# The order of two small matmuls on TensorE in a two-layer graph network: the mask's counting matmul and layer 1's second matmul

## The chip, the cores and the metric

The kernel runs on one core of one Trainium2 chip. The metric is the device time of one execution in microseconds. Of the kernel before there are three timed runs; the profile is one execution recorded by the hardware profiler.

## What is computed

128 batches of 128 nodes with 64 features go through two graph layers, each followed by a residual and a layer norm:

```python
# layer 0
mask = (adj > 0.0)
h   = relu((x @ W1a)[:, :, None, :] + (x[:, :, None, :] - x[:, None, :, :]) @ W1b + b1)   # (b, j, k, 192)
hm  = einsum('bjkh,bjk->bjh', h, mask)
x   = layernorm(x + hm @ W2 + mask.sum(-1)[..., None] * b2)
# layer 1
agg = einsum('bmn,bnd->bmd', adj, x)
h   = elu(agg @ V1 + c1)        # 64 -> 128
h   = elu(h @ V2 + c2)          # 128 -> 128
x   = layernorm(x + h @ V3 + c3)
```

About 6% of the mask's entries are set, so layer 0 doesn't have to look at all 128 x 128 pairs of nodes of a batch.

## The kernel before, in words

**Tiling.** Two batches are handled together as a pair p; there are 64 pairs and so 64 rounds. For each pair the nodes are sorted by their number of neighbours. The sorted nodes are cut into nine blocks with 7 to 22 slots per node, and each block is one unit of work: ScalarE writes a start value into a PSUM bank (L910), TensorE adds the neighbours' projections with 18 small matmuls (the gather, L920), and VectorE reduces the slots with absolute values (L930). Four banks `e0` to `e3` serve the units.

**The steps around the units.** Everything else of a pair is written as Python generators, whose steps yield an engine, a modelled cost, the events they need, and how many small PSUM banks they take:

- `turn` and `project_c` transpose the inputs and project the neighbours; the copy out of `turn`'s bank is `turned` (L695, ScalarE).
- `prepare` counts degrees and ranks the nodes. Its last step `permute` (L575, VectorE) frees its bank.
- `sort_x` and `project_a` sort the node features and project them (L606, TensorE); three ScalarE instructions write `aj` out of that bank (L613).
- `sort_mask` sorts the mask with a matmul, copies it as `mtp` (L659) and the permutation as `permT` (L661), then comes the counting matmul: `prefix` times `mtp` (L664 to L666; the helper `stationary`, L248, issues it), which numbers the set entries along each row. ScalarE copies the result as `vp` (L668), and VectorE compares it with slot numbers to make the one-hot tiles `oh` (L675) that the gather reads.
- `finish` is the rest of both layers of a pair: `hm` (L842), `project` (L847 and L851), the copy `ys` (L855), `unsort` (L864), a norm, `aggregate` (L871), layer 1's first matmul `hidden1` (L880), an elu (`r` L791, `e` L794, `h` L797), layer 1's second matmul `hidden2` (L886), a second elu, and `last` (L891 to L893) with the second norm.

**What sets the order.** The class `Flow` writes all engines' instructions out in one order. While the units run (all but the last 14 of 576), it always takes the runnable step with the smallest due time; a step is runnable when the steps that it needs have been written out and enough banks are free. The due times are in the table `DUE`: for pair p, a step's due time is `ROUND * p` plus its entry, with `ROUND = 11.1651`. Steps of several pairs so interleave in a fixed cycle. The entries of `sort_mask` are, in order, the sorting matmul, `mtp`, `permT`, the counting matmul, `vp`, and the nine `oh`. Those of `finish` have `hidden2` at 43.31 and the `r` behind it at 43.44.

In the last 14 units, and before the first gather, the step that can start first by the modelled clocks is taken, and due times only decide between near ones.

**Banks.** The small matmuls share four PSUM banks `m0` to `m3`. `give` appends a bank to a list when the step that reads it out has been written, and a matmul takes the first of the list:

```python
args = [self.free.pop(0)[1] for _ in range(banks)]
```

A matmul that writes a bank must wait on the chip until the instruction that last read it has ended. The framework puts these waits in by itself from the order of the instructions.

**PE mode.** A step marked `PE:*` follows the mode that TensorE is in: after a gather (mode "t") `stationary` issues two half-width matmuls, otherwise one of 128 columns.

Of the kernel before, what the change touches and what calls it, by code (L numbers as in the profile page):

```python
# [47 lines left out]
def gnn_kernel(ctx: ExitStack, tc: tile.TileContext, x, adj, w1, b1, w2, b2,  # L48
# [28 lines left out]
    with ExitStack() as fast:  # L77
        loads = fast.enter_context(tc.tile_pool(name="loads", bufs=8))
        prep = fast.enter_context(tc.tile_pool(name="prep", bufs=5))
        work = fast.enter_context(tc.tile_pool(name="work", bufs=5))  # L80
        ps_e = fast.enter_context(tc.tile_pool(name="ps_e", bufs=1, space=bass.MemoryType.PSUM))
        ps_m = fast.enter_context(tc.tile_pool(name="ps_m", bufs=1, space=bass.MemoryType.PSUM))
        K = sparse(tc, locals())
# [103 lines left out]
def sparse(tc, env):  # L187
# [17 lines left out]
    DUE = {  # L205
        "prepare": (-43.06, -42.93, -39.21, -39.08, -35.87),
        "sort_x": (-26.76, -10.46, -10.33, -3.14, -3.02, 2.5, 2.63, 2.76, 2.89),
        "sort_mask": (-26.12, -25.99, -25.86, -23.42, -23.29, -23.16, -13.67, -13.28, -13.03,
                      -12.77, -2.63, -2.25, -1.99, -1.73),
        "turn": (-36.9, -36.77),  # L210
        "project_c": (-32.15, -29.32, -29.2, -29.07, -28.94, -4.17, -4.04),
# [967 lines left out]
```

## Time and profile before

| | |
|---|---|
| timed runs, us | 758.67, 760.54, 761.2 |
| median, us | 760.54 |
| span of the profiled execution, us | 758.2 |
| its mean granted TensorE clock | 0.988 |
| the counting matmul (L248 with `prefix`), 64 times, mean ns | 273 |
| layer 1's second matmul (L886), 128 records for 64 steps, mean ns | 421 |
| copy `vp` (L668), 64 times, mean ns | 373 |

The span runs from the first to the last instruction of the program. The profiled execution is recorded apart from the list of times, and no time besides its span is given for it. FP32 matmuls appear as two records each, with a weight load before each. The end of a matmul in the profile is modelled, so successive matmuls seem to overlap; the starts tell more than the durations. PE is TensorE, PEld its weight loads, DVE VectorE, ACT ScalarE, POOL GpSimd. A line such as L248 is that of a helper, so the tile names tell the steps apart.

### The profile page before, as it was taken

The numbers are of one execution on the slowest core, as the hardware profiler recorded it, in microseconds if no ns is written. First come the engines' busy times: TensorE is split into PE (matmuls) and PEld (weight loads), VectorE is DVE, ScalarE is ACT, GpSimd is POOL, SyncE is SP. The second block draws the span as 40 slices with busy tenths as digits, with TensorE's granted clock in tenths as the row PEclk, the third lists the DMA queues.
The fourth block names the chain that finished last, engine by engine and source line by source line (L and its number), as shares of the span: only waits on it lengthen the run. The fifth ranks groups of instructions, "written<-read, shape, count | busy, mean of one in ns | idle before, by whom it ended". The sixth has DMA issues, their size and how long they took to land.

```text
span 758.2 us, 36118 instructions
## 1 busy us (share of the span) xinstructions
PE 736.3 (97%) x14788; PEld 672.4 (89%) x14789; DVE 722.5 (95%) x2381; ACT 705.7 (93%) x1986; POOL 432.4 (57%) x801
## 2 busy tenths in 40 slices
PE   7699999999999999999999999999999999999994
PEld 4588999999999999999999999999999999999993
DVE  7799999999999999999999999999999999999984
ACT  4499999999999999999999999999999999999984
POOL 5255566566556557556556656655655655655662
PEclk9799999999999999999999999999999999999998
DMA  4000011011011011011101101101101101100000
GB/s 121 15 3 3 17 31 31 17 31 32 16 31 32 20 27 31 20 27 31 28 20 31 31 17 32 31 16 31 31 20 28 31 21 27 31 21 16 10 13 19
DMA packets 54667, 19.72 MB, mean 26 GB/s; under 512 B 37600, under 2 KB 54496, under 8 KB 54496
## 3 DMA queue, kind: packets, MB, share of 16 engines
q1 hardware_dynamic: 53792, 17.05, 9.3%
q8 instruction: 118, 1.93, 1.1%
q14 instruction: 53, 0.43, 0.2%
q10 hardware_dynamic: 704, 0.30, 0.2%
HBM read 13.14 MB, written 4.19 MB: 23 GB/s over the span
## 4 chain that ended last, share of the span: by engine, by line
PE 95%; DVE 2%; ACT 1%; DMA 1%; issue 0%; POOL 0%; POOLq 0%; SPq 0%; DVEq 0%; ACTq 0%
PE e L920 46%; PE m L606 6%; PE m L708 5%; PE m L847 5%; PE m L886 4%; PE m L880 4%; PE m L893 4%; PE m L864 3%; PE m L246 3%; PE m L690 3%; PE m L592 2%; PE m L871 2%; PE m L851 1%; PE m L711 1%; PE m L248 1%; PE m L691 1%
## 5 line engine op out<-in xcount | busy, mean ns | idle before, releaser
L920 PE MATMUL e<-oh,cp 128*64 128x162 bf16 (+3 forms) x10368 | 393.3, 229 | 6.0 <-DVE oh L675 5.6
L920 PEld LDWEIGHTS <-cp 128*64 128x64 bf16 x10368 | 357.8, 110 | 18.3 <-issue 6.6
L930 DVE TENSOR_REDUCE sums<-e 128x54 f32<-128x486 f32 (+8 forms) x576 | 334.4, 608 | 10.2 <-PE e L920 4.6
L910 ACT COPY e<-aj 128x504 f32<-128x504 f32 (+6 forms) x576 | 293.6, 543 | 3.1 <-DVE sums L930 2.6
L749 POOL TENSOR_SCALAR ve<-st 128x2 f32<-128x2 f32 x126 | 24.1, 191 | 242.4 <-DVE st L742 237.0
L675 DVE TENSOR_TENSOR oh<-vp,slotc 128x308 bf16<-128x308 bf16 (+6 forms) x576 | 148.9, 315 | 4.8 <-ACT vp L668 1.3
L750 POOL TENSOR_TENSOR rs<-ve,mhalf 128x2 f32<-128x2 f32 x126 | 87.8, 697 | 10.5
L727 POOL TENSOR_TENSOR cp<-r,cp 128x512 bf16<-128x512 f32 x64 | 74.5, 1164 | 32.0 <-ACT cp L725 32.0
L642 POOL TENSOR_TENSOR corr<-ea,sa 128x384 f32<-128x384 f32 x64 | 64.3, 1005 | 16.5 <-DVE ea L635 11.5
L791 ACT ACTIVATE r<-m,cc 128x256 f32<-128x256 f32 x128 | 61.4, 480 | 5.2 <-PE m L880 3.2
L842 POOL TENSOR_TENSOR hm<-sums,corr 128x384 f32<-128x384 f32 x63 | 63.2, 1004 | 4.0 <-DVE sums L930 4.0
L620 POOL TENSOR_TENSOR sa<-aj,srow 128x384 f32<-128x384 f32 x64 | 64.3, 1005 | 1.0 <-ACT aj L613 1.0
L613 ACT ACTIVATE aj<-m,b1c 128x128 f32<-128x128 f32 x192 | 56.5, 366 | 8.2 <-PE m L606 1.2
L797 DVE SCALAR_TENSOR_TENSOR h<-m,cc,e 128x256 f32<-128x256 f32 x128 | 60.3, 471 | 2.0 <-ACT e L794 1.9
L794 ACT ACTIVATE e<-r 128x256 f32<-128x256 f32 x128 | 54.4, 426 | 2.1
L606 PE MATMUL m<-xsT,wad 128*128 128x128 f32 x384 | 53.7, 276 | 0.0
L847 PE MATMUL m<-w2d,hm 128*128 128x128 f32 x384 | 53.5, 276 | 0.0
L722 DVE TENSOR_TENSOR r<-m,cp 128x256 f32<-128x256 f32 x128 | 47.7, 414 | 1.6 <-ACT cp L718 1.6
L771 ACT ACTIVATE x<-y,nb,rs 128x64 f32<-128x64 f32 x126 | 49.0, 441 | 0.2 <-POOL nb L753 0.2
L718 ACT CAST cp<-m 128x256 bf16<-128x256 f32 x128 | 40.3, 366 | 8.8 <-PE m L711 8.8
L847 PEld LDWEIGHTS m<-w2d,hm 128*128 128x128 f32 x384 | 48.0, 192 | 0.3 <-POOL hm L842 0.3
L606 PEld LDWEIGHTS m<-xsT,wad 128*128 128x128 f32 x384 | 47.9, 192 | 0.4
(157 smaller groups left out, 1350.3 us busy)
## 6 DMA issues: line engine op xcount, KB each, us to landing
adj<-in_adj_dram SPq DMA_DIRECT2D x64, 128.0 KB, 2.9
xx<-in_x_dram SPq DMA_DIRECT2D x64, 64.0 KB, 2.6
out_dram<-o SPq DMA_DIRECT2D x64, 64.0 KB, 1.6
w1s<-in_L_gnn_W_dram ACTq DMA_DIRECT2D x2, 96.0 KB, 3.2
w2s<-in_L_gnn_W_dram ACTq DMA_DIRECT2D x2, 48.0 KB, 3.0
v2s<-in_L_gnn_W_dram SPq DMA_DIRECT2D x1, 64.0 KB, 2.2
v1d<-in_L_gnn_W_dram SPq DMA_DIRECT2D x2, 32.0 KB, 2.1
rows<-in_L_gnn_b_dram SPq DMA_DIRECT2D x1, 64.0 KB, 5.6
```

Source lines behind the costliest of these rows:

```text
L606: nc.tensor.matmul(aps[:, c * N:(c + 1) * N], wad[:, c, :], xsT, start=True, stop=True)
L620: evs, = yield ("POOL PORT", 1.0, [have] + made("srow"), 0, lambda: nc.gpsimd.tensor_mul(sa, aj, srow))
L642: ev, = yield ("POOL PORT", 1.05, [ev, evs], 0, lambda: nc.gpsimd.tensor_sub(corr, ea, sa))
L675: lambda: nc.vector.tensor_tensor(oh[:, :, c].rearrange("p b (s w) -> p b s w", w=w), vp[:, :, p0:p1].rearrange("p b (o w) -> p b o w", o= ...
L727: lambda: nc.gpsimd.tensor_sub(cp[:, 2], r1, cp[:, 1]))
L750: nc.gpsimd.tensor_tensor(rs, ve, mhalf, op=OP.pow)
L791: lambda: nc.scalar.activation(r, z, AF.Relu, bias=c, scale=-1.0))
L842: lambda: (nc.vector if late else nc.gpsimd).tensor_sub(hm, d["sums"], d["corr"]))
L847: nc.tensor.matmul(yb[:, :2 * O], hm[:, c, :], flat(w2d[:, c]), start=(c == 0), stop=False)
L910: lambda: nc.scalar.copy(e.rearrange("p (c s w) -> p c s w", c=3, w=w), d["aj"][:, :, p0:p1].rearrange("p c (o w) -> p c o w", o=1) .to_br ...
L920: nc.tensor.matmul(e[s * HB:(s + 1) * HB, c * n:(c + 1) * n], cp[:, k, s, c * HB:(c + 1) * HB], oh[:, s, base:base + n], start=False, stop ...
L930: nc.vector.tensor_reduce(d["sums"][:, :, p0:p1], e.rearrange("p (c s w) -> p c w s", c=3, w=w), AX.X, OP.add, apply_absolute_value=True)
```

## The change

One due time in the table of `sort_mask` is made smaller, that of the counting matmul:

```diff
     DUE = {
         "prepare": (-43.06, -42.93, -39.21, -39.08, -35.87),
         "sort_x": (-26.76, -10.46, -10.33, -3.14, -3.02, 2.5, 2.63, 2.76, 2.89),
-        "sort_mask": (-26.12, -25.99, -25.86, -23.42, -23.29, -23.16, -13.67, -13.28, -13.03,
+        "sort_mask": (-26.12, -25.99, -25.86, -23.75, -23.29, -23.16, -13.67, -13.28, -13.03,
                       -12.77, -2.63, -2.25, -1.99, -1.73),
```

For a pair p the counting matmul is now due at 11.1651 p - 23.75, and `hidden2` of pair p - 6 at 11.1651 p - 23.68 (43.31 - 6 x 11.1651 = -23.68). Before, it was due at 11.1651 p - 23.42, behind `hidden2` and behind that step's `r`. No other entry is changed, and no instruction is added or removed.

## The prediction

> **What bounds the kernel now.** I read the page first, then the table by windows, then the waits of the steady stretch, and last the order of time inside one round. The page:
>
> ```profile
> span 758.2 us, 36118 instructions
> PE 736.3 (97%) x14788; PEld 672.4 (89%) x14789; DVE 722.5 (95%) x2381; ACT 705.7 (93%) x1986; POOL 432.4 (57%) x801
> ...
> PE 95%; DVE 2%; ACT 1%; DMA 1%; issue 0%; POOL 0%; POOLq 0%; SPq 0%; DVEq 0%; ACTq 0%
> ```
>
> Four of five engines look full, but the chain that ended last is TensorE for 95% of the span. The windows were cut at 11.24 us, the distance from one round's instructions to the same ones of the next (64 rounds, one per pair of batches):
>
> ```profile
> 200.00:211.24 11.24, 11.24 (x238) 10.35 (x234) 11.06 (x37) 10.97 (x33) 6.65 (x13) 1.00 0.09 21
> ...
> 400.00:411.24 11.24, 11.24 (x239) 10.35 (x235) 11.07 (x37) 10.97 (x32) 6.64 (x13) 1.00 0.11 27
> ```
>
> After the length come the busy times of TensorE's matmuls (11.24 of 11.24), weight loads, VectorE, ScalarE, GpSimd, and the clock (1.00). TensorE has no free moment; VectorE has 0.17 us, ScalarE 0.27. The waits from 60 to 710 us, longest first:
>
> ```profile
> POOL ve L749 <- DVE st L742: 214.0, 57, 3.9
> POOL cp L727 <- ACT cp L725: 23.9, 58, 1.2
> PEld L711 <- issue: 19.2, 58, 0.3
> ```
>
> No matmul stands in that list. So a microsecond put on TensorE in a round is a microsecond on the span, once per round, and one taken off is won only if nothing else holds the matmul behind it. One round at the place of the change, in order of time (start, length, engine):
>
> ```profile
> 404.23 0.50 ACT L695 COPY turned<-m 128x384 f32<-128x384 f32 x1
> 404.85 0.88 ACT L613 ACTIVATE aj<-m,b1c 128x128 f32<-128x128 f32 x3
> 405.32 0.34 PE L851 MATMUL m<-cp,mtp 128*128 128x64 bf16 x6
> 405.46 0.30 PEld L886 LDWEIGHTS m<-h,v2s 128*128 128x128 f32 x2
> 405.49 0.68 PE L886 MATMUL m<-h,v2s 128*128 128x256 f32 x2
> 405.69 0.27 ACT L855 COPY ys<-m 128x128 f32<-128x128 f32 x1
> 405.79 0.10 PEld L248 LDWEIGHTS <-prefix 128*128 128x128 bf16 x1
> 406.01 0.27 PE L248 MATMUL m<-mtp,prefix 128*128 128x256 bf16 x1
> 406.01 0.52 PEld L864 LDWEIGHTS m<-ys,permT 128*128 128x128 f32 x4
> 406.12 0.56 PE L864 MATMUL m<-ys,permT 128*128 128x64 f32 x4
> 406.35 0.48 ACT L791 ACTIVATE r<-m,cc 128x256 f32<-128x256 f32 x1
> ```
>
> L886 is layer 1's second matmul (`hidden2`), L248 the counting matmul, L864 `unsort`. The same stretch in round 5, where no `hidden2` exists yet and the counting matmul already follows L851:
>
> ```profile
> 57.38 0.34 PE L851 MATMUL m<-cp,mtp 128*128 128x64 bf16 x6
> 57.53 0.10 PEld L248 LDWEIGHTS <-prefix 128*128 128x128 bf16 x1
> 57.56 0.27 PE L248 MATMUL m<-mtp,prefix 128*128 128x256 bf16 x1
> 57.76 0.27 ACT L855 COPY ys<-m 128x128 f32<-128x128 f32 x1
> 58.08 0.41 PEld L864 LDWEIGHTS m<-ys,permT 128*128 128x128 f32 x3 [0.45 <-ACT ys L855]
> ```
>
> It prices two things: the count's matmul can start about 0.03 us after L851's last, and a weight load held back by ScalarE starts 0.05 us after the ScalarE instruction ended (57.76 + 0.27 = 58.03, load at 58.08).
>
> [...] the count's load stands at 405.79 under the running L886, its matmul at 406.01, after it. So a waiting `hidden2` holds everything behind it. [...] bf16 loads of L851 come 0.03 us apart (six matmuls inside 0.17 us of the chain), L886's two FP32 loads 0.11 apart (405.46, 405.57). [...] So I reckon from starts alone.
>
> **The change part by part.** One due time moves, from -23.42 to -23.75 us of the kernel's own plan. Modulo the round of 11.1651 the counting matmul goes from 10.08 to 9.75; `hidden2` stands at 9.81, ScalarE's `r` of it at 9.94, the copy of unit 0 at 9.69. So it passes `hidden2` alone. No DMA and nothing of ScalarE, VectorE, GpSimd or SyncE changes place: `vp`, the count's eviction, stays behind `r`. The PE mode stays plain, since L847/L851 precede either way, so it stays one 128-column matmul (all 58 later records of L248 with `prefix` are). Swaps: round p against `hidden2` of p-6, so p = 6 to 63, 58 of them.
>
> *Streams.* Nothing is added or removed: `hidden2` 2 x 0.216 (its second matmul to the count's, 405.79 to 406.01), the count 0.11 (to L864's first, 406.12).
>
> *Weights.* Now `hidden2`'s first FP32 load starts behind a 64-column matmul and leaves TensorE uncovered: from 405.49 to the first L886 stream at 405.57, 0.08 us. Behind the count's 0.11 us stream the load would be covered. Gain at most 0.08. But L864's load needs `ys`, which ends at 405.96 and releases at 406.01; L864 starts its load exactly there now. So without any other effect the matmuls behind would not start earlier: 0.00 to -0.08 by itself, and I take 0.
>
> *The bank.* The four small PSUM banks are handed out first freed, first taken. The last four freed before this place are, by due time modulo the round, those of `turned` (7.89), `aj` (8.15), `ys` (8.40) and `permute` (8.79). Before, `hidden2` takes the first, the count the second. After, the count takes `turned`'s and `hidden2` takes `aj`'s. The trace supports it: L886's load and, separately, the count's matmul each wait for ScalarE's semaphore, and the second must be for something later than the first. `turned` ends at 404.23 + 0.50 = 404.73, long before either. `aj` ends at 404.85 + 0.88 = 405.73: harmless for a count at 406.01, late for a `hidden2` that would now load at 405.50. FP32 waits stand before the first weight load (L864 shows it in round 5), so the load is held too.
>
> Sum, round at 405 us:
> - the last L851 matmul starts at 405.46, the count at 405.49, its stream ends at 405.60;
> - `hidden2`'s load: 405.73 + 0.05 = 405.78;
> - first stream after the load's 0.11: 405.89; second 0.216 later: 406.11;
> - L864's first stream: 406.32 (its load at 406.11 or so, `ys` long there).
>
> Now it is 406.12. Cost about 0.207 us a round (unrounded starts), 0.19 if the release took 0.03, 0.22 if another hundredth or two comes on top. `aj` itself waits for TensorE (its PE source L606 ends right before it), so it moves with TensorE's clock and the loss repeats; it doesn't wear off.
>
> *Who waits behind.* On TensorE: L864, L880, the gathers of unit 8 and 0, all by 0.207. On ScalarE `r` starts now at 406.35, 0.18 after L886's modelled end (405.79 + 0.38); afterwards that end is 406.11 + 0.38 = 406.49, so `r` starts near 406.52, 0.16 late, less than TensorE's shift. `vp` behind it and `oh` on VectorE move by the same 0.16. Neither gains a stall against TensorE; both get slack.
>
> 58 x 0.207 = 12.0 us on the profiled span: 758.2 to 770.2. The fastest of the runs shown, 758.67, lies 0.5 above the span, the median of 760.54 2.3 above; the profiled execution is not marked among them. I add to the median: 772.5. In the last unit rounds (the final 14 units of 576) the order follows modelled ready times and could change a little; I put ±1 us on it.
>
> **Rivals.**
> *No bank wait, slack holds* (ends on the other side: not slower). If the banks went the other way round, or `aj` were free by 405.45, the swap would only hide the load. For: 0.08 us of uncovered load is really there. Against: `ys` pins L864 at 406.01, so 0 of it comes through; at most 58 x 0.08 = 4.6. Time 756 to 760.5. It decides if `aj` ended 0.28 us earlier than it does.
> *The wait holds the matmul, not its load.* Then the weights load under the count, the first stream starts near 405.78, second 406.00, L864 at 406.21: 0.10 a round, 5.6 us, 766. Against: L864's held load in round 5.
> *ScalarE and VectorE become the bound.* `hidden2`'s result comes 0.32 us later on the clock; with no slack before `r`, all of it would go round: 58 x 0.32 = 18.5, 779. Against: the 0.18 us before `r`, and VectorE's `oh` waits for ScalarE, which moves less than TensorE.
>
> **How the numbers follow.** Forecast 0.83 (770.5 to 774.5); matmul-only wait 0.05; larger bound 0.05; no bank wait 0.07. 0.3%, about 2.3 us, is what can be told from no change. Of the last case 0.05 falls within it and 0.02 below. Slower is 0.93. Range 769.0 to 774.8: the median's spread of runs (-1.9, +0.7), 0.19 to 0.22 a round (11.0 to 12.8) and the tail.
>
> **What would show it.** Right: rounds of 11.45 us; L248 with `prefix` before L886 and 0.03 after L851; L886's load 0.05 after the third `aj`; a wait of PE or its loads on `aj` L613, 58 times, near 0.2 to 0.3 us each; ScalarE and VectorE busy the same microseconds in a longer round. Wrong: rounds of 11.24 (no bank wait), of 11.34 (load not held), of 11.5 and more (a second engine bound), or L248 in two halves.

## The result, and the profile after

The changed kernel takes 771.55 us (median of five runs, 770.46 to 773.13), the kernel before in the same comparison 759.63 (758.67 to 761.2). The ratio is 1.0157, with a 95% interval of 1.0142 to 1.0173: 11.9 us slower, where 12.0 was forecast.

The page of the changed kernel, span, busy times and the chain that ended last:

```profile
span 768.7 us, 36118 instructions
PE 745.6 (97%) x14788; PEld 675.3 (88%) x14789; DVE 723.2 (94%) x2381; ACT 710.2 (92%) x1986; POOL 432.2 (56%) x801
...
PE 95%; DVE 2%; ACT 1%; issue 1%; DMA 0%; POOL 0%; ACTq 0%; POOLq 0%; DVEq 0%
```

The instructions are as many as before, and the chain still lies on TensorE. The table by windows, cut at the new length of a round:

```profile
200.00:211.44 11.44, 11.42 (x238) 10.42 (x234) 11.06 (x37) 11.04 (x33) 6.65 (x13) 1.00 0.12 31
400.00:411.44 11.44, 11.42 (x234) 10.42 (x232) 11.07 (x38) 11.05 (x31) 6.66 (x12) 1.00 0.11 25
```

VectorE does the same 11.06 to 11.07 us of work as in a round of 11.24; the round around it is 0.20 longer. TensorE, with no free moment before, now has 0.02 free in this account. That is far less than it lost, since the modelled ends of matmuls reach into the gap: the count's recorded end is at 410.69 in the order of time below, its stream is over at 410.53 by estimate (410.42 + 0.11, the 0.11 from the kernel before, where `unsort`'s first matmul follows the count's from 406.01 to 406.12). The waits between 60 and 720 us show it better:

```profile
POOL ve L749 <- DVE st L742: 223.2, 57, 4.0
POOL cp L727 <- ACT cp L725: 26.5, 58, 1.2
PEld L711 <- issue: 19.2, 58, 0.3
DVE oh L675 <- ACT vp L668: 13.0, 56, 0.3
PEld m L886 <- ACT aj L613: 12.6, 57, 0.2
```

The fifth line is new: the weight load of layer 1's second matmul waits for `aj`, 57 times, 0.22 us each. The fourth is a consequence: VectorE's `oh` waits for `vp`, which ScalarE writes behind `r`, which needs the second matmul. One round in order of time:

```profile
409.16 0.50 ACT L695 COPY turned<-m 128x384 f32<-128x384 f32 x1
...
409.77 0.89 ACT L613 ACTIVATE aj<-m,b1c 128x128 f32<-128x128 f32 x3
...
410.25 0.34 PE L851 MATMUL m<-cp,mtp 128*128 128x64 bf16 x6
410.39 0.10 PEld L248 LDWEIGHTS <-prefix 128*128 128x128 bf16 x1
410.42 0.27 PE L248 MATMUL m<-mtp,prefix 128*128 128x256 bf16 x1
...
410.62 0.27 ACT L855 COPY ys<-m 128x128 f32<-128x128 f32 x1
410.71 0.30 PEld L886 LDWEIGHTS m<-h,v2s 128*128 128x128 f32 x2 [0.22 <-ACT aj L613]
410.71 0.70 PE L886 MATMUL m<-h,v2s 128*128 128x256 f32 x2
411.04 0.63 PEld L864 LDWEIGHTS m<-ys,permT 128*128 128x128 f32 x4
411.25 0.55 PE L864 MATMUL m<-ys,permT 128*128 128x64 f32 x4
411.45 0.47 ACT L791 ACTIVATE r<-m,cc 128x256 f32<-128x256 f32 x1
```

`aj` ends at 409.77 + 0.89 = 410.66, and the load starts 0.05 later. Between the end of the count's stream (410.42 + 0.11) and L886's first stream (410.82 by estimate, 0.11 after its load at 410.71; its second load starts there, 0.216 before its second matmul at 411.03) TensorE has nothing to stream for 0.29 us; before, it was 0.08 at this place (405.49 to 405.57). The difference is the round's loss.

The profiled span grew by only 10.5 us. The missing microsecond isn't part of the change. From the first `unsort` load behind a swapped pair to that step's last record in round 63 it is 68.8 to 709.4 us before and 67.7 to 719.9 after, 640.6 against 652.2: 11.6 more. The start up to round 6, whose order is the same, was 1.1 us shorter in the changed kernel's profile. This goes with the clock granted there (third column from the right, 0.79 and 0.94; the kernel before first, then the changed one):

```profile
30.00:40.00 10.00, 9.54 (x192) 8.76 (x190) 7.62 (x21) 7.44 (x20) 2.15 (x2) 0.79 0.01 2
30.00:40.00 10.00, 9.54 (x220) 8.07 (x218) 8.60 (x25) 8.54 (x22) 2.79 (x3) 0.94 0.01 2
```

All eleven profiles of this document agree: where the clock of these 10 us is 0.78 or 0.79 (three of them), the fourth counting matmul starts at 37.6 to 38.2 us, and where it is 0.86 to 0.94, at 36.2 to 36.6. The order of before is on both sides (0.79 here, 0.93 with the one-instruction `aj` below), so it isn't the change.

### The profile page after: what moved, and what is told of

Same layout as the page of the kernel before. It is cut to its first block, busy times and chain, and to the rows that moved or that the text cites. A ratio compares the mean times of both kernels' runs of the same rounds, so it can differ in the third digit from the quotient of the medians.

```text
span 768.7 us, 36118 instructions
## 1 busy us (share of the span) xinstructions
PE 745.6 (97%) x14788; PEld 675.3 (88%) x14789; DVE 723.2 (94%) x2381; ACT 710.2 (92%) x1986; POOL 432.2 (56%) x801
## 4 chain that ended last, share of the span: by engine, by line
PE 95%; DVE 2%; ACT 1%; issue 1%; DMA 0%; POOL 0%; ACTq 0%; POOLq 0%; DVEq 0%
PE e L920 46%; PE m L886 6%; PE m L606 6%; PE m L708 5%; PE m L847 5%; PE m L880 4%; PE m L893 4%; PE m L864 3%; PE m L246 3%; PE m L690 3%; PE m L592 2%; PE m L871 2%; PE m L851 1%; PE m L711 1%; PE m L248 1%; PE m L691 1%
## 5 line engine op out<-in xcount | busy, mean ns | idle before, releaser
L750 POOL TENSOR_TENSOR rs<-ve,mhalf 128x2 f32<-128x2 f32 x126 | 87.8, 697 | 10.5
L642 POOL TENSOR_TENSOR corr<-ea,sa 128x384 f32<-128x384 f32 x64 | 64.3, 1004 | 16.5 <-DVE ea L635 11.5
L613 ACT ACTIVATE aj<-m,b1c 128x128 f32<-128x128 f32 x192 | 56.6, 366 | 8.1 <-PE m L606 1.2
```

Of the source, the lines that this page charges most:

```text
L642: ev, = yield ("POOL PORT", 1.05, [ev, evs], 0, lambda: nc.gpsimd.tensor_sub(corr, ea, sa))
L750: nc.gpsimd.tensor_tensor(rs, ve, mhalf, op=OP.pow)
```

## Experiments

The round is the distance from one counting matmul to the next in the profile, median. Ratios are against the kernel before, which ran beside each: its median was 759.12 us beside the four runs after the changed kernel, 759.0 beside the three with the one-instruction `aj`, and 759.16 beside the last two.

| kernel | median us | ratio, 95% interval | round us |
|---|---|---|---|
| before (first comparison) | 759.63 | 1 | 11.240 |
| changed | 771.55 | 1.0157 (1.0142 to 1.0173) | 11.444 |
| second matmul on `permute`'s bank | 766.28 | 1.0093 (1.0078 to 1.0109) | 11.357 |
| second matmul on `ys`'s bank | 784.91 | 1.0347 (1.0331 to 1.0362) | 11.667 |
| order of before, banks exchanged | 776.8 | 1.0228 (1.0213 to 1.0244) | 11.553 |
| order of before, first matmul ahead of `unsort` | 756.79 | 0.9972 (0.9961 to 0.9984) | 11.187 |
| one-instruction `aj`, order of before | 759.82 | 1.0005 (0.9996 to 1.0014) | 11.240 |
| one-instruction `aj`, changed order | 759.0 | 1.0002 (0.9993 to 1.0010) | 11.237 |
| the same, first matmul ahead of `unsort` | 752.48 | 0.9917 (0.9903 to 0.9932) | 11.104 |
| `permute` early, first matmul ahead of `unsort` | 752.61 | 0.9922 (0.9909 to 0.9936) | 11.104 |
| `permute` early | 759.03 | 0.9997 (0.9989 to 1.0006) | 11.237 |

**The changed order with other banks.** Three banks are free when the second matmul takes one: those of `aj`, `ys` and `permute`, in this order. The edit lets it take another than the first where three are free:

```diff
+    PICK = {'hidden2': 2}
+    HAVE = {'hidden2': 3}
...
-                args = [self.free.pop(0)[1] for _ in range(banks)]
+                k = self.PICK.get(fn.__name__, 0) if self.under_way and len(self.free) == self.HAVE.get(fn.__name__) else 0
+                args = [self.free.pop(k)[1] for _ in range(banks)]
```

> The changed order is kept; only the bank that layer 1's second matmul takes is another: the one that the VectorE step permute (L575) frees, not the one of aj. In the profile of the changed kernel permute ends 0.18 us after the last L851 matmul starts, aj 0.27 us after. Theory (the wait for the bank's last reader, in front of the weight load, is the whole loss): L886's load starts 0.05 us after permute, 0.23 instead of 0.32 us after L851; 0.116 us a round over the kernel before in place of 0.207, 58 rounds: 6.7 us, about 766.3 us, and a wait of L886's load on L575. Rival (the order itself costs, by the later result of the second matmul on ScalarE and VectorE): no difference to the changed kernel, about 771.6 us.

Measured: 766.28 us, and a round 0.117 longer than before (0.116 expected). The order of time in this kernel:

```profile
407.88 0.41 DVE L575 TENSOR_TENSOR permb<-m,pos 128x256 bf16<-128x256 f32 x1
407.96 0.34 PE L851 MATMUL m<-cp,mtp 128*128 128x64 bf16 x6
...
408.35 0.30 PEld L886 LDWEIGHTS m<-h,v2s 128*128 128x128 f32 x2
```

The load follows `permute`'s end (407.88 + 0.41) by 0.06, by 0.05 in the median of 57 rounds. The list of waits hardly shows it (L575 twice between 80 and 700 us): the weight loads pause for only 0.14 us here (408.11 + 0.10 to 408.35). The order is that of the changed kernel; about 5 us of the loss went with the bank alone.

The other way, with the index 1 in place of 2:

> The changed order is kept; layer 1's second matmul takes the bank that the copy ys (L855) frees, which ends later than aj (0.50 us after L851's last matmul starts). Theory (bank wait): its load starts at 0.55 us, the two streams end at 1.09 us, L864 follows there against 0.653 before: 0.434 us a round, 58 rounds: 25.2 us, about 785 us. Rival (order itself): about 771.6 us, as the order is the same.

Measured: 784.91 us, a round 0.427 longer (0.434 expected).

```profile
417.54 0.27 ACT L855 COPY ys<-m 128x128 f32<-128x128 f32 x1
...
417.85 0.30 PEld L886 LDWEIGHTS m<-h,v2s 128*128 128x128 f32 x2 [0.45 <-ACT ys L855]
```

With three banks in one and the same order the loss follows the end of the bank's last reader: 0.12, 0.20 and 0.43 us a round. The order as the cause in itself is out.

**The wait without the change of order.** The kernel before with `PICK = {'hidden2': 1}` and `HAVE = {'hidden2': 4}`, so that the second matmul, in front as ever, takes `aj`'s bank and the count `turned`'s.

> The order of the kernel before, with the two banks exchanged: layer 1's second matmul, still in front, takes the bank of aj, the counting matmul that of turned. Theory (bank wait): the load of L886 stands at 0.32 us after L851's last matmul, its streams end at 0.86, the count's at 0.97, where L864 starts, against 0.653: 0.315 us a round, 18.3 us, about 778 us, so more than the change costs, as the count no longer fills part of the wait. Rival (order itself): no change, 759.6 us.

Measured: 776.8 us, a round 0.313 longer (0.315 expected).

```profile
413.28 0.88 ACT L613 ACTIVATE aj<-m,b1c 128x128 f32<-128x128 f32 x3
...
414.21 0.30 PEld L886 LDWEIGHTS m<-h,v2s 128*128 128x128 f32 x2 [0.25 <-ACT aj L613]
```

So the wait alone costs 0.31, and the order that the change brings makes it cheaper by 0.11 (0.313 less 0.204), the length of the count's stream (406.01 to 406.12 in the kernel before), which now runs inside the wait.

**The reading of TensorE's starts.** A due time that has nothing to do with the change:

```diff
-        "finish": (12.64, 19.44, 19.57, 21.62, 21.75, 21.88, 22.01, 28.04, 28.17, 29.2, 33.56,
+        "finish": (12.64, 19.44, 19.57, 21.62, 21.75, 21.88, 22.01, 28.04, 28.17, 29.2, 32.53,
```

> Not the change: in the order of the kernel before, layer 1's first matmul (L880) is put in front of unsort (L864) by its due time alone (32.53 in place of 33.56). By the reading that TensorE's starts alone set the round: L880's first weight load is then no longer uncovered behind a 64-column matmul (0.165 in place of 0.112 us), 0.055 us a round less, 3.2 us, about 756.5 us. It takes the bank of ys, free at 0.55 us after L851, when its load is due at 0.55, so a loss of a few hundredths would show if that is late. Rival (VectorE at 11.07 and ScalarE at 10.97 of 11.24 us are as much the bound): no gain or a loss.

Measured: 756.79 us, a round 0.053 shorter (0.055 expected). Before, L880's first load started at 406.45, 0.055 us after `unsort`'s last matmul, and its second 0.11 later. Here its first load starts with the count's matmul at 402.81, and its first matmul 0.11 later at 402.92, when the count's stream ends. From the count's matmul to the next gather it is 1.04 us (402.81 to 403.85), 1.09 before (406.01 to 407.10), and the round takes all of it; VectorE and ScalarE follow (11.12 and 10.98 us busy in a window of 11.24). In 57 or 58 rounds this makes 3.1 us; the medians differ by 2.3 (759.12 and 756.79), and the end of the last experiment shows where a part went.

**What holds the gain back.** In these three runs `aj` is done by one instruction. It leaves out two of the three bias columns, so these kernels do not compute the whole function:

```diff
-            for c in range(3):
-                nc.scalar.activation(aj[:, c, :], aps[:, c * N:(c + 1) * N], AF.Identity,
-                                     bias=b1c[:, c:c + 1])
+            nc.scalar.activation(flat(aj), aps[:, :3 * N], AF.Identity, bias=b1c[:, 0:1])
```

> Order of the kernel before. Part of the computation is changed: aj is written by one ScalarE instruction over all 384 columns with the first bias column, in place of three instructions with a bias column each, so two thirds of the layer-0 bias are the wrong ones and ScalarE is done about 0.3 us earlier. It is the base for the two runs beside it. Every theory: TensorE bound as before, about 759.6 us.

> Changed order, with the same one-instruction aj (wrong bias for two thirds). aj then ends before the second matmul's load is due. Theory (bank wait, and ys as the next thing in the way): no wait on aj is left, but L864's load still waits for ys, so the covered weight load is worth nothing: equal to the run with the one-instruction aj in the order before, 0.0 us within 1. Rival 1 (order itself): 12 us slower than that run. Rival 2 (ys does not hold L864): 58 x 0.08 = 4.6 us faster.

Measured: 759.82 and 759.0 us. Some 0.3 us less work on ScalarE in a round (10.63 us in a window of 11.24, 10.97 before) changes nothing in the old order, and with it the new order costs nothing. The waits of the second of them, between 60 and 700 us:

```profile
ACT ys L855 <- PE m L851: 15.0, 57, 0.3
PEld m L864 <- ACT ys L855: 12.1, 57, 0.2
```

No line names `aj`. In its place `unsort`'s load waits for `ys`, 0.21 us each time: the covered weight load was won and handed to the next wait.

> As the one-instruction aj in the changed order (wrong bias for two thirds), and layer 1's first matmul (L880) between the second (L886) and unsort (L864), with the bank of permute, so that L864 comes late enough for ys. Theory (ys was what kept the covered load from paying): 0.08 for L886's load and 0.055 for L880's load a round, 7.9 us faster than the one-instruction aj in the order before, if VectorE (11.06 us busy a round) can follow into a round of 11.10; 4 to 8 us. Rival (the cover is worth nothing whatever ys does): 3.2 us, L880's part alone.

Here the second matmul stays behind the count, the first matmul fills the time until `ys`, and takes `permute`'s bank by the same kind of index. Measured: 752.48 us and a round of 11.104, 0.136 shorter. With the old order the same move of the first matmul gave 0.053; the further 0.083 is the covered load of the second matmul (0.08 uncovered before, 405.49 to 405.57). `ys` was what kept it from paying.

**A version that keeps the whole computation.** The bank can be freed early by a due time, too:

```diff
-        "prepare": (-43.06, -42.93, -39.21, -39.08, -35.87),
+        "prepare": (-43.06, -42.93, -39.21, -39.08, -36.56),
```

> The whole computation. Changed order, and permute (L575) early as in the run beside it, nothing else. Theory (bank wait, then ys): the wait of L886's load is gone, L864's load waits for ys: the round of the kernel before, 11.24 us, about 759 us. Rival (order itself): about 771 us. Rival (ys does not matter): 0.08 us a round faster than before, about 754.5 us.

Measured: 759.03 us, the time of before, with this line among its waits:

```profile
PEld m L864 <- ACT ys L855: 11.9, 56, 0.2
```

With the first matmul's due time at 32.53 as well:

> The whole computation. Changed order, and by due times alone: permute (L575) before the VectorE one-hot steps (-36.56 in place of -35.87), so that its bank is freed ahead of aj's and goes to layer 1's second matmul, and layer 1's first matmul (L880) before unsort (L864) (32.53 in place of 33.56). permute then starts about 0.62 us before L851's last matmul starts and ends 0.2 us before it; neither L886 nor L880 should wait for a bank, and L864 no longer for ys. Theory: 0.08 + 0.055 = 0.136 us a round less than the kernel before, as the run with the one-instruction aj showed (11.104 us a round): 7.9 us, about 751.5 us, if ScalarE, which here has the three-instruction aj and 10.97 us of work a round, follows. Rival (ScalarE or VectorE is the bound by now): between 752 and 757 us.

Measured: 752.61 us, 0.9922 of the kernel before: 5.9 us faster than it by this ratio, 6.5 by the medians, and 19 us faster than the changed one, from three due times (the changed one among them). The order of time:

```profile
398.99 0.41 DVE L575 TENSOR_TENSOR permb<-m,pos 128x256 bf16<-128x256 f32 x1
398.99 0.88 ACT L613 ACTIVATE aj<-m,b1c 128x128 f32<-128x128 f32 x3
399.35 0.33 PEld L851 LDWEIGHTS <-mtp 128*128 128x128 bf16 x6
399.46 0.34 PE L851 MATMUL m<-cp,mtp 128*128 128x64 bf16 x6
399.61 0.10 PEld L248 LDWEIGHTS <-prefix 128*128 128x128 bf16 x1
399.64 0.27 PE L248 MATMUL m<-mtp,prefix 128*128 128x256 bf16 x1
399.64 0.30 PEld L886 LDWEIGHTS m<-h,v2s 128*128 128x128 f32 x2
399.75 0.60 PE L886 MATMUL m<-h,v2s 128*128 128x256 f32 x2
399.84 0.27 ACT L855 COPY ys<-m 128x128 f32<-128x128 f32 x1
399.97 0.63 PEld L880 LDWEIGHTS m<-agg,v1p 128*128 128x128 f32 x4
```

L886's load starts with the count's matmul, and the matmul itself 0.11 later, at the moment when the count's stream ends: no gap. Its table by windows, TensorE's matmuls full again and VectorE close behind:

```profile
400.00:411.10 11.10, 11.10 (x233) 10.36 (x232) 11.01 (x38) 10.86 (x32) 6.68 (x12) 1.00 0.11 27
```

The round of 11.104 is the expected one, so ScalarE and VectorE do not bound it. The time is 1.1 us above the expected 751.5, though, and inside the range that the rival had. The rounds are not what is missing: from the count of round 6 to that of round 63 it is 632.6 us in the profile, 640.2 before. But from the last count to the end it is 51.7 us, 49.2 before. The 5 us that begin 35 us after the last count, before and now (the clock is again the third column from the right):

```profile
744.03:749.03 5.00, 3.69 (x33) 2.85 (x32) 3.27 (x12) 3.19 (x9) 1.40 (x3) 1.00 0.06 13
733.99:738.99 5.00, 4.34 (x28) 3.75 (x28) 2.26 (x11) 2.24 (x8) 1.52 (x3) 0.61 0.07 15
```

So some 2.5 us of the gain are lost behind the rounds, where the granted clock is lower and the order of TensorE's last steps is another too (`hidden1` ahead of `unsort`). Which of the two it is, isn't shown. The other two kernels with `hidden1` early have 50.6 us (old order) and 51.3 (one-instruction `aj`) behind the last count, the eight without it 49.2 to 50.3.

## Why the prediction was right

**The bound.** That TensorE alone sets the round was read from 11.24 busy us in 11.24 and the missing matmul among the waits. The run with the first matmul ahead of `unsort` shows it from the other side: 0.053 us taken off TensorE came off the round.

**The banks.** That the second matmul would get `aj`'s bank was derived from the due times and from two separate waits on one semaphore, that of L886's load at 405.46 and that of the count's matmul at 406.01. The new wait names L613. Two other banks in the changed order and the exchanged banks in the old order gave three other losses, each within 0.01 us of its sum. In all four the load of L886 starts 0.04 to 0.06 us after the end of the bank's last reader: 410.66 to 410.71 behind `aj` in the changed kernel, 408.29 to 408.35 behind `permute`, 417.81 to 417.85 behind `ys`, 414.16 to 414.21 behind `aj` in the order of before.

**The sum.** Load at 0.32 us after L851's last matmul: in the window above 410.71 against 410.39, the count's load, which starts with that matmul. L864's first matmul at 0.86: 411.25 less 410.39. Per round 0.204 us in place of 0.207, and 58 of them make 11.8; the ratio says 11.9. The forecast of 772.5 lies 0.9 above the median because it stood on 760.54, the median of three runs, and the five runs of the comparison have 759.63.

**Who waits behind.** `r` was to come 0.16 us late: it starts 1.06 us after L851's last matmul (411.45 less 410.39), 0.89 before (406.35 less 405.46), so 0.17. L864 was held along with L886: its load comes 0.148 us after the end of `ys` in the median round, 0.051 before. ScalarE and VectorE did not become the bound (11.05 and 11.07 us busy in the window of 11.44). The listed wait of `oh` on `vp` is slack in the longer round.

**The rivals.** No bank wait: `aj` had to end 0.28 us earlier, and with the one-instruction `aj`, which ends before, the loss is gone. That the gain then is 0 and not 4.6 us, because of `ys`, was taken on an argument, and two runs bear it out (ratios 1.0002 and 0.9997): in both, as in the kernel before, `unsort`'s load starts 0.051 us after the end of `ys` in the median round. A wait that holds the matmul and lets its weights through: the wait stands on the load, and L864 is at 0.86 and not 0.75. A second engine as the bound: rounds of 11.44, not 11.5 and more (58 x 0.32 there is 18.6, not 18.5; the 779 stands). The change did what it says: L248 with `prefix` still is one 128-column matmul in 58 records.

What stays open is small: why the clock granted between 30 and 40 us differs from profile to profile.

## What to carry to other kernels

When buffers are handed out first freed, first taken, moving a step in the order also exchanges its buffer with the step it passes, and the wait that comes with the buffer is not in the diff: list the last releases before the place and ask who gets which. Then price the wait from the end of the buffer's last reader (the load followed it by some 0.05 us here), not from the data the step needs. And where a covered load should bring a gain, look at what is late next: here it was the copy `ys`, for which `unsort`'s load then waited 0.21 us, and only a third step put in between let the gain through.

## What was not expected of the hardware

How exactly the times add up. From single rows of the kernel before, a release of 0.05 us from a ScalarE end to the weight load (58.03 to 58.08; taken for VectorE as well, where `permute`'s bank then showed 0.05 in the median), a load of 0.11 (405.46 to 405.57) and streams of 0.216 and 0.11 (405.79 to 406.01 to 406.12), the losses of four arrangements (the changed kernel and the three runs with other banks) were expected at 0.116, 0.207, 0.315 and 0.434 us a round and measured at 0.117, 0.204, 0.313 and 0.427. The recorded busy time of TensorE is no such measure: of the 0.20 us that a round lost, the windows show 0.02 as free.
